# Layer norm roots in a macaron block: shift and Newton steps in place of ScalarE's square root

## The chip, the cores and the metric

The kernel runs on one core of a Trainium2 chip. The metric is the device time of one execution in microseconds (us). A core has five engines with an instruction stream of their own: TensorE (PE in the profile, with PEld for its weight loads), VectorE (DVE), ScalarE (ACT), GpSimd (POOL) and SyncE (SP), which issues most transfers.[...]

## The reference, cut to what matters

The block is a macaron: half a feed-forward network, causal attention, half a feed-forward network, each with a residual, on 8 sequences of 512 rows and 128 columns, all in float32. Each of the three parts begins with a layer norm, and the feed-forward part has a second one of its own directly behind the first.

```python
def _layernorm(x, eps=1e-05):
    m, v = mean(x, -1), var(x, -1)
    return (x - m) / sqrt(v + eps)

def ffn(x):                                  # 8 experts, 2 taken for each row
    xn = (x - mean(x)) * rsqrt(var(x) + eps) * ln_gamma + ln_beta
    abel = gelu(xn @ abel_w + abel_b)
    w = softmax over the top 2 of (xn @ gate_w + gate_b)
    moe = sum_e w[e] * (gelu(xn @ ew1[e] + eb1[e]) @ ew2[e] + eb2[e])
    for i in range(3): moe = moe @ expm(gens[i])
    gate = sigmoid([abel, moe] @ gc_w + gc_b)
    return x + abel * (1 - gate) + moe * gate

x = x + 0.5 * ffn(_layernorm(x))
x = x + attention(_layernorm(x))             # 16 heads of 8, causal, a bias by distance
x = x + 0.5 * ffn(_layernorm(x))
```

For each row the feed-forward part needs two roots of the same variance v: 1/sqrt(v + eps) for the outer norm, and 1/sqrt(v(1 + eps) + eps^2) for the two norms together. Attention needs the first alone. There are 8 x 512 rows, and each of the three parts takes its roots from new values of x.

## The kernel before, in words

A sequence is kept as a tile of 128 rows by 4 by 128 columns (`xs[b]`), so the statistics of one sequence are 4 numbers in each of the 128 partitions. The program has these stages, with the time that each begins in the profiled execution:

- 0 us, the prologue (`f_first`). `f_stats(0, ...)` makes the statistics of sequences 0 to 3 and then of 4 to 7 in one piece each (16 columns of variances). For each sequence `f_norm` normalises on VectorE (line 322), `f_turn` turns the tile on TensorE and scales it on ScalarE (lines 187 and 344), and `f_logits` makes the routing logits (`pl`, line 184). `f_sort` sorts rows by expert on VectorE, and `f_send` writes them to memory with indirect transfers that GpSimd issues (line 468). Between these runs `rotation_steps`, a chain of small matrix products (`rq`, `rc`, `rp`) that builds the matrix exponentials. TensorE's instructions are pinned to the order in which they are written (`mm`, `tp`, lines 183 to 187).
- 113 us, records of the experts' weights, and from 132 us the experts of sequences 0 to 3 (`f_experts(0, 0)`), their mixing (`f_fetch` with line 599's indirect transfers, `f_mix`), and the experts of sequences 4 to 7. Beside these last experts stand `statistics((0,), "o")` and `statistics((1,), "p")`, the attention norms of the first two sequences (the dictionary in `between`).
- 300 us, attention. One loop runs over slots; a unit is four heads of one sequence, 32 units of 12 slots. In each slot TensorE makes one score tile in each of two layouts: `sa`, of which VectorE takes the row maxima (line 925), and, 20 slots later for the same unit, `sb`, of which ScalarE takes exponentials (line 964). GpSimd zeroes what lies behind the diagonal (line 969, `affine_select`), and TensorE weighs the values (`py`). There are three buffers each of `sa` and `sb`, and two for everything else in TensorE's output memory. The dictionary `todo` puts other work into slots. `statistics` for sequences 2 to 7 ("q") is in slot 60. When a sequence is done, its feed-forward norm is put at 14 slots from there: `f_stats(1, (b,))` at 14, `f_norm` at 15 (on ScalarE, line 326), `f_turn` at 19, `f_half` at 21 and `f_logits` at 22. This is done for sequences 0 to 6, and the sends of group 0 follow on sequence 3's logits.
- 790 us, the second feed-forward part (`f_second`), which begins with `f_stats(1, (7,))` and then runs experts, fetches and mixing for both groups.

In `f_stats` the variances come from VectorE (lines 302 and 304), the two square roots from ScalarE (lines 305 and 306), the reciprocal of both, minus the mean times the root (`nm`) and two coefficients for the residual (`cf`) from VectorE again (lines 307 to 311). `statistics` has the same with one square root (lines 821 to 823). `f_norm`, `normalise` and `f_half` read these as scale and bias.

On ScalarE a function of another table set needs a load of the set. The square root is in a set that holds neither the exponential nor the gelu, so around each square root the program has a load before it and one behind it. A call to `pin` keeps the order among the instructions of an engine that are so marked; the rest is put in order by a scheduler of the framework.

Of the kernel before, what the change touches and what calls it, by code (L numbers as in the profile page):

```python
# [8 lines left out]
F32 = mybir.dt.float32  # L9
I32 = mybir.dt.int32  # L10
AF = mybir.ActivationFunctionType
ALU = mybir.AluOpType
# [4 lines left out]
P = 128  # L17
NB, S = 8, 512
# [6 lines left out]
EPS = 1e-5  # L25
# [31 lines left out]
def tile_macaron(  # L57
# [20 lines left out]
    V, A, G, T = nc.vector, nc.scalar, nc.gpsimd, nc.tensor  # L78

    const = ctx.enter_context(tc.tile_pool(name="const", bufs=1))  # L80
    stat = ctx.enter_context(tc.tile_pool(name="stat", bufs=2))
# [55 lines left out]

    ident = const.tile([P, P], F32, name="ident", tag="ident")
    make_identity(nc, ident)
    eps_c = const.tile([P, 1], F32, name="eps_c", tag="eps_c")  # L140
    G.memset(eps_c, EPS)
    eps2_c = const.tile([P, 1], F32, name="eps2_c", tag="eps2_c")
    G.memset(eps2_c, EPS * EPS)

    eye2 = early.tile([P, 2, P], F32, name="eye2", tag="eye2")
    for i in range(2):
# [34 lines left out]
    pin = tc.keep_in_program_order  # L181
# [105 lines left out]
    xTs = [const.tile([P, S], F32, name=f"xT{b}", tag=f"xT{b}") for b in range(NB)]  # L287
    made, xhs_f = {}, {}

    def f_stats(n, bs):  # L290


        name = f"{n}_{bs[0]}"
        w = len(bs) * TT
        st = stat.tile([P, w, 6], F32, name=f"st{name}", tag=f"st{w}")
        mv = stat.tile([P, w, 2], F32, name=f"mv{name}", tag=f"mv{w}")
        rs = stat.tile([P, 2, w], F32, name=f"rs{name}", tag=f"rs{w}")
        nm = stat.tile([P, w], F32, name=f"nm{name}", tag=f"nm{w}")
        cf = stat.tile([P, 2, w], F32, name=f"cf{name}", tag=f"cf{w}")
        for i, b in enumerate(bs):  # L300
            for t in range(TT):
                V.bn_stats(st[:, i * TT + t, :], xs[b][:, t, :])
        for t in range(w):
            V.bn_aggr(mv[:, t, :], st[:, t, :])
        A.activation(rs[:, 0, :], mv[:, :, 1], AF.Sqrt, bias=eps_c)
        A.activation(rs[:, 1, :], mv[:, :, 1], AF.Sqrt, bias=eps2_c, scale=1.0 + EPS)
        V.reciprocal(rs, rs)
        V.scalar_tensor_tensor(nm, mv[:, :, 0], -1.0, rs[:, 1, :], ALU.mult, ALU.mult)

        V.tensor_scalar(cf[:, 0, :], rs[:, 0, :], 0.5, 1.0, ALU.mult, ALU.add)  # L310
        V.scalar_tensor_tensor(cf[:, 1, :], mv[:, :, 0], -0.5, rs[:, 0, :], ALU.mult, ALU.mult)
        for i, b in enumerate(bs):
            made[n, b] = (rs, nm, cf, i * TT)
# [316 lines left out]
    def f_first(between):  # L630

        with ExitStack() as ph:
# [13 lines left out]
            groups = [tuple(range(g * GROUP, (g + 1) * GROUP)) for g in range(2)]  # L646
            go(1)
            f_stats(0, groups[0])
            go(2)
            for b in groups[0]:  # L650
# [6 lines left out]
            for b in groups[0]:  # L657
                f_half(0, b)
            go(1)
            f_stats(0, groups[1])  # L660
            go(1)
            for b in groups[1]:
# [37 lines left out]
    def f_second():  # L700

        with ExitStack() as ph:
            pools = f_pools(1, ph)
            n, b = 1, NB - 1
            sides = {b: f_beside(n, b, pools["hid"], pools["misc"], pools["sb"]) for b in range(NB)}

            def side(b):
                next(sides[b], None)

            tasks = {  # L710
                0: [(f_norm, n, b)],
                1: [(f_turn, n, b, pools["misc"])],
                2: [(f_logits, n, b, pools["misc"])],
                3: [(f_sort, n, 1, pools["misc"])],
                4: [(f_send, n, i, t) for i in range(GROUP, NB) for t in range(TT)],
                5: [(f_half, n, b)],
            }
            for i in range(NB):
                tasks.setdefault(5 + 2 * i, []).append((side, i))
                tasks.setdefault(6 + 2 * i, []).append((side, i))  # L720
            f_stats(n, (b,))
            f_experts(n, 0, pools, tasks)
            for b in range(GROUP):
                for t in range(TT):
                    f_fetch(n, b, t, pools["sb"], 2)
                f_mix(n, b, True)
            f_experts(n, 1, pools, {})
            for b in range(GROUP, NB):
                for t in range(TT):
                    f_fetch(n, b, t, pools["sb"], 2)  # L730
                f_mix(n, b, True)
# [78 lines left out]
    def statistics(bs, name):  # L810
        w = len(bs) * TT
        st = stat.tile([P, w, 6], F32, name=f"cst{name}", tag=f"cst{name}", bufs=1)
        mv = stat.tile([P, w, 2], F32, name=f"cmv{name}", tag=f"cmv{name}", bufs=1)
        rs = stat.tile([P, w], F32, name=f"crs{name}", tag=f"crs{name}", bufs=1)
        nm = stat.tile([P, w], F32, name=f"cnm{name}", tag=f"cnm{name}", bufs=1)
        for i, b in enumerate(bs):
            for t in range(TT):
                V.bn_stats(st[:, i * TT + t, :], xs[b][:, t, :])
        for t in range(w):
            V.bn_aggr(mv[:, t, :], st[:, t, :])  # L820
        A.activation(rs, mv[:, :, 1], AF.Sqrt, bias=eps_c)
        V.reciprocal(rs, rs)
        V.scalar_tensor_tensor(nm, mv[:, :, 0], -1.0, rs, ALU.mult, ALU.mult)
        for i, b in enumerate(bs):
            norms[b] = (rs, nm, i * TT)
# [58 lines left out]
    def attention():  # L884
# [4 lines left out]
        with ExitStack() as ph:  # L889
# [152 lines left out]
            for k in range(GROUP * TT):  # L1042
                b, t = GROUP + k // TT, k % TT
                at(2 + 3 * k, f_fetch, 0, b, t, work, 1)
                if t == TT - 1:
                    at(4 + 3 * k, f_mix, 0, b, False)
            before(1, NG * FILLS - 27)
            at(60, statistics, tuple(range(2, NB)), "q")
            for b in range(2, NB):
                before(b, b * NG * FILLS - 29)  # L1050
# [33 lines left out]
    def between(psum):  # L1084

        return {
            10: [(statistics, (0,), "o"), (normalise, 0)],
            13: [(turn, 0, psum)],
            15: [(spread, 0, 0, psum)],
            16: [(spread, 0, 1, psum)],  # L1090
            18: [(values, 0, psum)],
            20: [(statistics, (1,), "p")],
        }
# [87 lines left out]
```

## Time and profile before

| | |
|---|---|
| median of three runs | 1016.43 us (1006.78 to 1019.03) |
| the profiled execution's own time | 1012.17 us |
| its span, first to last instruction | 1010.1 us |
| mean granted TensorE clock | 0.860 |
| busy: TensorE, VectorE, ScalarE, GpSimd | 800.7, 546.6, 446.9, 348.7 us |
| table loads on ScalarE | 28, each 1.283 us (10 of them at line 305, 9 at line 964, 3 at line 821) |
| square roots on ScalarE | 23, of 0.28 to 0.32 us |

How to read the rows that follow: a row of the timeline has its start, its duration, the engine, the line, the operation, output and inputs by name, their shapes, how many instructions it holds, and in brackets the idle time before it with what ended it. A row of groups has the busy time, the mean of one in ns and then the idle time before. A row of windows has the window, its length, the busy time and the number of instructions of PE, PEld, DVE, ACT and POOL, and then the granted clock, the share of the DMA engines and GB/s.

### The profile page before, as it was taken

How to read it: one execution, taken by the hardware profiler on the slowest of the kernel's cores; microseconds unless marked ns; L12 is line 12 of the kernel's file. 1: busy time of each engine (PE TensorE's matmuls, PEld its weight loads, DVE VectorE, ACT ScalarE, POOL GpSimd, SP SyncE). 2: the span in 40 equal slices, each digit the busy share in tenths (PEclk: the TensorE clock that was granted, in tenths of full speed). 3: DMA queues.
4: the chain of work that ended last, by engine and by line, in shares of the span. 5: the costliest groups of instructions: out<-in, count | busy, mean ns of one | idle time of the engine just before them, and what ended most of it. 6: DMA issues, size and time to landing. Idle time of an engine off the chain costs nothing.

```text
span 1010.1 us, 17346 instructions
## 1 busy us (share of the span) xinstructions
PE 800.7 (79%) x5546; PEld 554.1 (55%) x5546; DVE 546.6 (54%) x2049; ACT 446.9 (44%) x928; POOL 348.7 (35%) x421
## 2 busy tenths in 40 slices
PE   4569888767668689999999967999999779956800
PEld 4469777656545345555555533455655578845800
DVE  5855533254338565676767672676773253445323
ACT  2434233235203355767676732666766434412300
POOL 4277700245034521121212138332111047074075
PEclk9579989978766777999999975999999789978955
DMA  9973166756621300101010101201000346766622
GB/s 259 299 188 75 56 224 221 217 158 178 159 71 25 69 14 11 36 4 43 4 44 3 44 17 49 56 10 42 4 3 2 107 148 217 248 178 179 218 58 68
DMA packets 104010, 101.22 MB, mean 100 GB/s; under 512 B 11424, under 2 KB 80936, under 8 KB 103640
## 3 DMA queue, kind: packets, MB, share of 16 engines
q1 hardware_dynamic: 95728, 83.26, 28.5%
q0 software_dynamic: 8192, 16.86, 6.0%
q8 instruction: 44, 0.72, 0.3%
q14 instruction: 46, 0.38, 0.1%
HBM read 34.37 MB, written 32.89 MB: 67 GB/s over the span
## 4 chain that ended last, share of the span: by engine, by line
PE 65%; DMA 8%; issue 7%; POOL 7%; DVE 7%; SPq 3%; ACT 2%; POOLq 0%; DVEq 0%; ACTq 0%
PE sa L184 18%; PE sb L184 9%; PE py L184 8%; POOL ye L599 6%; PE ph L184 6%; PE po L184 6%; DMA ye<-yd,to 4%; DMA xr<-xd 3%; PE rp L184 3%; PE pl L184 2%; PE pyt L187 2%; PE px L187 2%; PE pp L184 2%; SPq L509 1%; PE ab L184 1%
## 5 line engine op out<-in xcount | busy, mean ns | idle before, releaser
L925 DVE CUSTOM_DVE_ANT_0 junk<-sa,mask_q 128x128 f32<-128x128 f32 (+3 forms) x512 | 251.1, 490 | 146.1 <-PE sb L184 96.4
L184 PE MATMUL sa<-ks,qs 32*128 32x128 f32 (+3 forms) x1024 | 289.9, 514 | 15.4 <-DVE mx L925 15.2
L184 PE MATMUL sb<-qs,ks 32*128 32x256 f32 (+3 forms) x1024 | 284.8, 502 | 5.5 <-DMA qs<-mr 5.5
L964 ACT ACTIVATE pr<-sb 128x384 f32<-128x384 f32 (+1 forms) x384 | 188.6, 524 | 153.9 <-PE sb L184 142.7
L599 POOL DMA_INDIRECT ye<-yd,to x128 | 123.1, 961 | 239.5 <-DMA r<-rec 68.9
L184 PEld LDWEIGHTS sa<-ks,qs 32*128 32x128 f32 x1024 | 126.6, 203 | 117.8 <-DVE mx L925 88.4
L969 POOL TENSOR_SCALAR_AFFINE_SELECT pr<-pr 128x512 f32<-128x512 f32 x128 | 80.0, 637 | 302.5 <-ACT pr L964 302.4
L468 POOL DMA_INDIRECT xd<-xh,to x128 | 125.3, 979 | 110.3 <-issue 34.6
L546 ACT ACTIVATE hs<-ph,r 128x256 f32<-128x256 f32 x184 | 82.7, 474 | 151.9 <-PE ph L184 143.4
L184 PEld LDWEIGHTS sb<-qs,ks 32*128 32x128 f32 x1024 | 136.1, 199 | 18.3 <-issue 8.1
L184 PE MATMUL ph<-xs,r 128*128 128x256 f32 x368 | 113.5, 438 | 38.2 <-issue 24.4
L184 PEld LDWEIGHTS po<-r,hs 128*128 128x128 f32 x736 | 105.2, 208 | 6.0
L184 PE MATMUL po<-r,hs 128*128 128x129 f32 x736 | 104.5, 290 | 0.0
L184 PEld LDWEIGHTS ph<-xs,r 128*128 128x128 f32 x368 | 74.1, 224 | 48.4 <-issue 40.1
L184 PE MATMUL py<-pr,va 128*32 128x512 f32 (+3 forms) x1024 | 94.8, 469 | 2.8 <-POOL pr L969 2.8
L561 DVE TENSOR_TENSOR y<-po,r 128x258 f32<-128x258 f32 x92 | 39.0, 424 | 80.3 <-PE po L184 65.9
L532 DVE TENSOR_SCALAR xs<-px,cs 128x256 f32<-128x256 f32 x92 | 49.6, 541 | 53.9 <-PE px L187 51.5
L613 DVE TENSOR_TENSOR ye<-ye,wts 128x516 f32<-128x516 f32 x32 | 22.0, 696 | 91.2 <-DMA ye<-yd,to 91.2
L187 PE MATMUL px<-ident,xr 128*128 128x128 f32 x184 | 40.7, 308 | 38.0 <-DMA xr<-xd 32.3
L620 ACT ACTIVATE gt<-gt,half_gcb 128x4 f32<-128x4 f32 x16 | 4.7, 296 | 114.9 <-DVE gt L619 114.9
L184 PEld LDWEIGHTS py<-pr,va 128*32 128x32 f32 x1024 | 24.4, 112 | 53.9 <-issue 23.0
L187 PEld LDWEIGHTS px<-ident,xr 128*128 128x128 f32 x184 | 24.1, 156 | 50.2 <-issue 31.8
(185 smaller groups left out, 850.2 us busy)
## 6 DMA issues: line engine op xcount, KB each, us to landing
r<-rec SPq DMA_DIRECT2D x92, 322.5 KB
yd<-y SPq DMA_DIRECT2D x92, 129.0 KB
xr<-xd SPq DMA_DIRECT2D x92, 128.0 KB
xd<-blank SPq DMA_DIRECT2D x2, 2944.0 KB
qkd<-qk SPq DMA_DIRECT2D x16, 256.0 KB
x<-in_x_dram SPq DMA_DIRECT2D x8, 256.0 KB
qs<-in_alibi_q_dram SPq DMA_DIRECT2D x2, 1024.0 KB
ks<-in_alibi_k_dram SPq DMA_DIRECT2D x2, 1024.0 KB
```

The lines of the kernel that those rows point to most:

```text
L184: pin(T.matmul(*args, **kw))
L187: pin(T.transpose(*args))
L468: d = G.indirect_dma_start(out=xd[g], out_offset=bass.IndirectOffsetOnAxis(to[:, k, j : j + 1], 0), in_=xhs_f[n, b][:, t, :], in_offset=None,)
L509: e = nc.sync.value_load(whose[0:1, t : t + 1], min_val=0, max_val=NE - 1)
L532: V.tensor_scalar(xT, pt.rearrange("p c q -> p (c q)"), cs[:, C_GAMMA : C_GAMMA + 1], cs[:, C_BETA : C_BETA + 1], ALU.mult, ALU.add,)
L546: A.activation(got[t][3][:, c, :], ph[:, :SLOTS], AF.Gelu, bias=r[:, E_B1 + c : E_B1 + c + 1])
L561: V.tensor_tensor(y, po, r[:, E_B2:RECORD].unsqueeze(1).to_broadcast([P, CHUNKS, PO]), ALU.add)
L599: pin(G.indirect_dma_start(out=back[b][k][:, t, :], out_offset=None, in_=yd[g], in_offset=bass.IndirectOffsetOnAxis(to[:, k, j : j + 1], 0),))
L613: V.tensor_tensor(ys[k], ys[k], wts[:, k, js].unsqueeze(2).to_broadcast([P, TT, PO]), ALU.mult)
L925: V.tensor_tensor_reduce(junk[:, :n], sa[:, at : at + n], mask_q[:, S - n :], 1.0, -3.0e38, ALU.add, ALU.max, mxs[u][:, j, i : i + 1],)
L964: A.activation(pr[:, j, :], sb[:, :width], AF.Exp)
L969: pin(G.affine_select(out=pr[:, :, at : at + P], in_=pr[:, :, at : at + P], pattern=[[0, GH], [1, P]], compare_op=ALU.is_ge, fill=0.0, bas ...
```

## The change

Both square roots go. A new helper, `inverse_root`, takes the variance with eps added and makes 1/sqrt of it: it shifts the number's bits right by one, takes that from the constant 1597463007 (as a multiplication by -1 and an addition, into an integer), and reads the bits as a number again. Three Newton steps follow, each y = y(1.5 - 0.5 v y^2), written as four instructions. The two integer instructions are on VectorE always. The twelve others are on VectorE too, or, where `late` is set, on GpSimd and pinned there. `late` is set for `f_stats(1, (b,))` with b from 0 to 6, the seven calls within attention. The constant tiles `eps_c` and `eps2_c` go, as do the reciprocals; eps is added by a `tensor_scalar` on VectorE. In `statistics` the result is copied into `rs`.

```diff
-    eps_c = const.tile([P, 1], F32, name="eps_c", tag="eps_c")
-    G.memset(eps_c, EPS)
-    eps2_c = const.tile([P, 1], F32, name="eps2_c", tag="eps2_c")
-    G.memset(eps2_c, EPS * EPS)
...
+    def inverse_root(v, name, late):
+        shape, key = list(v.shape), "x".join(str(d) for d in v.shape[1:])
+        y = stat.tile(shape, F32, name=f"iy{name}", tag=f"iy{key}")
+        t = stat.tile(shape, F32, name=f"it{name}", tag=f"it{key}", bufs=1)
+        V.tensor_scalar(y.bitcast(I32), v.bitcast(I32), 1, None, ALU.logical_shift_right)
+        V.tensor_scalar(y.bitcast(I32), y.bitcast(I32), -1.0, 1597463007.0, ALU.mult, ALU.add)
+        E, keep = (G, pin) if late else (V, lambda i: i)
+        for _ in range(3):
+            keep(E.tensor_tensor(t, y, y, ALU.mult))
+            keep(E.tensor_tensor(t, t, v, ALU.mult))
+            keep(E.tensor_scalar(t, t, -0.5, 1.5, ALU.mult, ALU.add))
+            keep(E.tensor_tensor(y, y, t, ALU.mult))
+        return y
...
     def f_stats(n, bs):
...
-        rs = stat.tile([P, 2, w], F32, name=f"rs{name}", tag=f"rs{w}")
+        ve = stat.tile([P, 2, w], F32, name=f"ve{name}", tag=f"ve{w}", bufs=1)
...
-        A.activation(rs[:, 0, :], mv[:, :, 1], AF.Sqrt, bias=eps_c)
-        A.activation(rs[:, 1, :], mv[:, :, 1], AF.Sqrt, bias=eps2_c, scale=1.0 + EPS)
-        V.reciprocal(rs, rs)
+        V.tensor_scalar(ve[:, 0, :], mv[:, :, 1], 1.0, EPS, ALU.mult, ALU.add)
+        V.tensor_scalar(ve[:, 1, :], mv[:, :, 1], 1.0 + EPS, EPS * EPS, ALU.mult, ALU.add)
+        rs = inverse_root(ve, f"f{name}", n == 1 and len(bs) == 1 and bs[0] < NB - 1)
...
     def statistics(bs, name):
...
-        A.activation(rs, mv[:, :, 1], AF.Sqrt, bias=eps_c)
-        V.reciprocal(rs, rs)
+        V.tensor_scalar(ve, mv[:, :, 1], 1.0, EPS, ALU.mult, ALU.add)
+        rs = stat.tile([P, w], F32, name=f"crs{name}", tag=f"crs{name}", bufs=1)
+        V.tensor_copy(rs, inverse_root(ve, f"c{name}", False))
```

More of the change, by code (lines that the diff above doesn't have):

```diff
@@ L813, in statistics @@
         mv = stat.tile([P, w, 2], F32, name=f"cmv{name}", tag=f"cmv{name}", bufs=1)
-        rs = stat.tile([P, w], F32, name=f"crs{name}", tag=f"crs{name}", bufs=1)
+        ve = stat.tile([P, w], F32, name=f"cve{name}", tag=f"cve{name}", bufs=1)
         nm = stat.tile([P, w], F32, name=f"cnm{name}", tag=f"cnm{name}", bufs=1)
```

## The prediction

> **What bounds the kernel now.** I read the page's summary and chain first, then the stages, then every place where a square root stands.
>
> ```profile
> PE 800.7 (79%) x5546; PEld 554.1 (55%) x5546; DVE 546.6 (54%) x2049; ACT 446.9 (44%) x928; POOL 348.7 (35%) x421
> PE 65%; DMA 8%; issue 7%; POOL 7%; DVE 7%; SPq 3%; ACT 2%; POOLq 0%; DVEq 0%; ACTq 0%
> ```
>
> TensorE makes 65% of the chain, ScalarE 2%: work taken off ScalarE is worth little unless TensorE waits for it. By stage:
>
> ```profile
> core 0: us, PE busy (x) PEld busy (x) DVE busy (x) ACT busy (x) POOL busy (x), PEclk, DMA share, GB/s
> 400.00:580.00 180.00, 180.00 (x1484) 100.62 (x1483) 123.55 (x519) 125.45 (x259) 36.87 (x56) 1.00 0.11 26
> 640.00:790.00 150.00, 149.98 (x1232) 83.00 (x1230) 91.92 (x384) 99.59 (x206) 35.43 (x53) 0.99 0.08 19
> ```
>
> In attention TensorE is full at full clock. Seven of the ten layer norm roots stand there, one for each of sequences 0 to 6. The trace around one of them:
>
> ```profile
> 411.65 1.28 ACT L305 ACT_TABLE_LOAD   x1
> 412.19 0.36 DVE L304 BATCH_NORM_AGGREGATE mv<-st 128x2 f32<-128x6 f32 x4
> 412.94 0.30 ACT L305 ACTIVATE rs<-mv,eps_c 128x4 f32<-128x4 f32 x1
> 413.44 1.28 ACT L964 ACT_TABLE_LOAD   x1
> 413.66 0.20 DVE L307 RECIPROCAL rs<-rs 128x8 f32<-128x8 f32 x1
> 413.89 0.16 DVE L308 SCALAR_TENSOR_TENSOR nm<-mv,rs 128x4 f32<-128x4 f32 x1
> 414.74 0.60 ACT L964 ACTIVATE pr<-sb 128x512 f32<-128x512 f32 x1
> 415.23 1.64 ACT L326 ACTIVATE xh<-x,nm,rs 128x128 f32<-128x128 f32 x4
> ```
>
> The first load overlaps VectorE's variances; nm is ready at 414.05, but xh starts only at 415.23, behind the second load and an exponential. ScalarE is shut to exponentials from 411.65 to 414.72. At sequence 6 this reaches TensorE:
>
> ```profile
> 760.19 0.29 PEld L184 LDWEIGHTS sb<-qs,ks 32*128 32x128 f32 x2 [0.34 <-ACT pr L964]
> 761.07 0.42 PEld L187 LDWEIGHTS pt<-ident,xh 128*128 128x128 f32 x4 [0.59 <-ACT mr L937]
> ```
>
> ```profile
> 758.60:762.10 3.50, 3.50 (x17) 1.73 (x16) 1.54 (x10) 3.24 (x10) 0.74 (x2) 1.00 0.00 0
> 762.10:765.50 3.40, 3.40 (x32) 2.09 (x30) 0.57 (x2) 1.52 (x3) 0.29 (x1) 0.50 0.04 7
> ```
>
> The clock column falls from 1.00 to 0.50 for 3.4 us after these short waits: attention has little slack there.
>
> **The change part by part.** *Removed:* 24 of 28 table loads (4 are left in the built program) and 23 square roots, 24 x 1.28 + 23 x 0.30 = 38 us of ScalarE. Some of it already reaches TensorE: its waits on ScalarE around the seven roots are some 1.3 us at six of them and 2.9 at sequence 6, 10.7 us in all, the most that quick roots can return. *Added:* thirteen chains of two integer operations and 12 Newton steps: six chains wholly on VectorE (the two groups of the prologue, sequence 7, and the three of statistics), seven with their 12 steps on GpSimd. TensorE's order stays as it was, and SyncE's transfers only swap among neighbours.
>
> *Prologue.* The roots of sequences 4 to 7 are on the chain:
>
> ```profile
> 43.55 1.07 DVE L304 BATCH_NORM_AGGREGATE mv<-st 128x2 f32<-128x6 f32 x15
> 45.52 0.33 DVE L307 RECIPROCAL rs<-rs 128x32 f32<-128x32 f32 x1
> 45.88 0.18 DVE L308 SCALAR_TENSOR_TENSOR nm<-mv,rs 128x16 f32<-128x16 f32 x1
> 46.82 0.87 PE L187 MATMUL pt<-ident,xh 128*128 128x128 f32 x3 [3.81 <-DVE xh L322]
> ```
>
> Here the square roots cost nothing: they ran at 44.65 to 45.16 beside three rotation products on VectorE. In their place come 16 dependent VectorE operations of 0.19 (the 128x32 row of lg) + 0.035 of spacing (413.86 to 413.89) = 3.6 us, less 0.35 for the reciprocal: +3.1 (a little of it may hide). For sequences 0 to 3, six of the steps are put ahead of VectorE's copies that TensorE's first rotation products wait for at 11.23: +1.1. TensorE is full behind this (37.69 of 38 us from 75 to 113), so +4.2 stays.
>
> *Attention, seven times.* VectorE: two scalings and two integer operations, 4 x 0.165, end 0.65 after mv, about 413.2 (no shift of integers is in the trace; the nearest rows with an int32 result are 0.167 and 0.206, so 0.65 to 0.8). Then come a hand-over of 0.1, 12 steps of price p on GpSimd, a hand-over back, nm (0.16) and the hand-over to ScalarE: xh starts at 413.6 + 12p, in place of 415.23. No tiny arithmetic on GpSimd is in the trace; the nearest rows:
>
> ```profile
> L835 POOL TENSOR_TENSOR x<-x,rw 128x512 f32<-128x512 f32 x8 | 10.2, 1279 | 0.0
> L755 POOL TENSOR_SCALAR_AFFINE_SELECT steps_q<-steps_q 32x512 f32<-32x512 f32 x1 | 0.6, 604 | 0.0
> L151 POOL TENSOR_SCALAR_AFFINE_SELECT mask_q<-mask_q 128x128 f32<-128x128 f32 x1 | 0.3, 283 | 0.0
> ```
>
> From 604 and 283 ns for 512 and 128 columns follows 176 ns at no columns; 8 columns at the tensor_tensor's 2.15 ns each make 0.19, with VectorE's spacing p = 0.225, 12p = 2.7, and xh is 1.1 later: 7 x 1.1 = +7.8. Below, the memset of one column took 97 ns: p = 0.10 gives -0.4 each, -2.6 in all. Above, p = 0.30 gives +2.0 each, +14. I take 0.225, the rows nearest in kind. The Trainium skill (GPSIMD Engine Reference, 4.1 Engine selection) speaks against this placing: elementwise work belongs on VectorE, being about twice as slow on GpSimd for two inputs. Twice VectorE's row here (0.165) is p = 0.33 and +2.4 each, +17 in all; but that factor is of long rows, and in these the start of an operation is nearly all, so the rows decide.
>
> The new wait is nm's: VectorE stands some 2.7 us for GpSimd. Behind it are queued cf, the four va additions and the score maxima (L925) of the next sa tiles; TensorE waits for these when the three sa buffers are used up, and turns xh only after xh. ScalarE meanwhile does the exponentials that it could not do before; xh is queued in front of later ones, so they wait too. GpSimd itself is not behind: the affine_select that follows the chain waited 6.59 us for ScalarE at 415.46, and only sequence 4's chain has a send (0.98 us) just before it. This cover holds the stall to about xh's shift; without it up to 2.5 us each would show.
>
> *The clock.* Stalls of 2 us come in each of the seven places; before, the one of this size was followed by a half-clock window of 3.4 us, worth 1.7. Half of the six others: 3 x 1.7 = +5.1 (ends 0 and 10.2). The Trainium skill (TensorE: Matmul & The Clock Gate, Why this matters for your kernels) asks only for gaps under about 3 us; by it this term is 0 and the total 12.5. The row at 762.10 fell after gaps under 0.6 us each, so I keep it.
>
> *The rest.* In statistics "o" and "p" lie beside gathers and mixing: +0.25. "q" gives exponentials 2.6 us and takes 3.4 us of VectorE in a stretch with idle engines: 0 (-1 to +1). The last f_stats, on VectorE: nm 0.8 later, xh mostly hidden by expert products: +0.3 (0.2 to 0.8). If the exponentials' freed time returned one third of the 10.7, that would be -3.6; I don't count it, since nm's wait stands in the same place.
>
> Sum: 4.2 + 7.8 + 5.1 + 0.25 + 0.3 = +17.6. Against the profiled execution's own 1012.17 (span 1010.1 and 2.1 around it) that is 1029.8; against the median shown, 1016.43, it is 1034.0. I say 1032. About 2%, 20 us, is what a measurement of this kernel can tell from no change: faster is under 996.1, slower over 1036.8.
>
> **The rivals.** *Main, 0.42:* as summed, 1032; its own range is 1020 (p = 0.15, no clock) to 1045 (p = 0.30, all six windows). *The clock stays down, 0.28:* after a wait of 3.86 us at 366.57 the clock was half from 366.1 to 390.0, 24 us, worth 12. If the stalls of nm add to the waits for sa and xh so that one window falls under what sequence 6 had, each such place costs 12 in place of 1.7; two or three of seven make 17.6 + 18 to 36, some 1050. The point: TensorE stands more than about 3 us in one place. For it: at sequence 6 it was near already. Against it: many weights stay ready ahead. *Cheap steps, 0.22:* p about 0.15, no new half-clock windows: 4.2 + 1.6 + 0.8 = +6.6, 1021. *A gain, 0.08:* p = 0.10 and the freed ScalarE returns the 10.7: 4.5 - 10.7 = -6, 1010. For it: exponentials really are shut out for 3.1 us each time; against it: xh waits for a longer chain. That the loads stay is excluded, since the built program has four.
>
> The range 1011 to 1052 leaves out half of the gain and somewhat under half of the slow rival, 0.16. Slower by over 2%: all of the rival and a third of the main case, 0.41; faster by over 2% needs more than everything returned, 0.02; within 0.57.
>
> **What would show it.** ScalarE with 4 table loads; the GpSimd steps with their mean (0.19 expected) and VectorE's nm waiting 2.7 us on GpSimd seven times; the first pl of sequence 4 at about 53.6 in place of 49.37; weight loads of pt and sa waiting 1 to 2 us after each f_stats; in 400 to 790, a few 3.4 us windows at half clock. Wrong if p is far from 0.2, if TensorE's pt is far enough behind xh to hide the shift, or if half-clock stretches come of the moved timing alone.

## The result, and the profile after

The changed kernel took 1059.12 us (median of four, 1054.67 to 1064.83), the kernel before beside it 1011.61: a ratio of 1.0467, interval 1.037 to 1.0563. It is slower by 47 us where 16 to 18 were forecast, and lies above the stated range. Medians are of all runs of a kernel, but ratios and intervals, here and below, compare only those within 1.5% of the kernel's fastest, so a ratio can differ from that of the two medians. The profiled execution has a span of 1058.1 us and a mean clock of 0.831 (before 0.860).

The page's summary, its chain by engine, and from the groups of ScalarE the table loads of the kernel after:

```profile
PE 827.3 (78%) x5546; PEld 571.6 (54%) x5546; DVE 564.8 (53%) x2160; ACT 411.4 (39%) x881; POOL 365.1 (34%) x503
PE 60%; POOL 10%; DVE 9%; DMA 9%; issue 8%; ACT 2%; SPq 1%; POOLq 0%; DVEq 0%; ACTq 0%
```

```profile
L215 ACT ACT_TABLE_LOAD x1 | 1.3, 1283 | 0.8 <-PEq L1177 0.8
L496 ACT ACT_TABLE_LOAD x1 | 1.3, 1283 | 0.0
L977 ACT ACT_TABLE_LOAD x1 | 1.3, 1283 | 0.0
L558 ACT ACT_TABLE_LOAD x1 | 1.3, 1283 | 0.0
```

The change did what it says: four loads are left, and ScalarE is 35 us less busy. TensorE, with the same instructions, is 27 us more busy. The two stages of attention that were full at full clock before, in the table by stage of the kernel after:

```profile
400.00:580.00 180.00, 173.81 (x1340) 97.57 (x1344) 113.71 (x473) 102.50 (x221) 40.84 (x87) 0.91 0.09 20
640.00:790.00 150.00, 142.65 (x1085) 78.41 (x1085) 89.91 (x375) 78.00 (x165) 55.12 (x90) 0.87 0.11 27
```

The granted clock fell from 1.00 and 0.99 to 0.91 and 0.87, and TensorE now has gaps there. Laying the same TensorE instruction of both traces side by side shows where the time is lost: 8.0 us by 71 us (the prologue), 4.0 from 390 us of the kernel before to sequence 0's root (a stretch at half clock in front of that took 13.7 us and not 23.9), 44.9 at the end of sequence 7, 48 at the end. So attention lost 40.8 us, and it did so at each of the seven roots (3.6 to 8.2 us). One of them, in the timeline of the kernel after:

```profile
416.25 0.36 DVE L316 BATCH_NORM_AGGREGATE mv<-st 128x2 f32<-128x6 f32 x4
...
417.12 0.17 DVE L293 TENSOR_SCALAR iyf<-iyf 128x8 int32<-128x8 int32 x1
...
417.38 0.20 POOL L296 TENSOR_TENSOR itf<-iyf 128x8 f32<-128x8 f32 x1 [4.46 <-DVE iyf L293]
417.65 0.20 POOL L297 TENSOR_TENSOR itf<-itf,ve 128x8 f32<-128x8 f32 x1
...
420.49 0.20 POOL L299 TENSOR_TENSOR iyf<-iyf,itf 128x8 f32<-128x8 f32 x1
420.65 0.64 POOL L982 TENSOR_SCALAR_AFFINE_SELECT pr<-pr 128x512 f32<-128x512 f32 x1
420.73 0.57 DVE L320 SCALAR_TENSOR_TENSOR nm<-mv,iyf 128x4 f32<-128x4 f32 x1 [2.84 <-POOL iyf L299]
...
421.33 1.65 ACT L338 ACTIVATE xh<-x,nm,iyf 128x128 f32<-128x128 f32 x4 [3.60 <-DVE nm L320]
421.37 0.87 DVE L889 TENSOR_TENSOR va<-pv,rw 128x128 f32<-128x128 f32 x4
...
422.35 0.09 PEld L183 LDWEIGHTS pm<-ident,mx 128*16 128x16 f32 x1 [2.10 <-issue]
...
422.38 0.27 PE L183 MATMUL pm<-ident,mx 128*16 128x128 f32 x1 [1.73 <-DVE va L889]
```

Twelve steps on GpSimd, each 0.20 long and 0.283 from the next, take 3.31 us. VectorE stands 2.84 us for them, and nm itself takes 0.57 in place of 0.16. From the end of mv to the end of nm it is 4.69 us (before 1.50, from 412.55 to 414.05). Behind nm stand the four va additions, and for the last of them pm waits, the transpose of the maxima. It doesn't wait for maxima: those that it turns were finished at 417.9. It waits for a buffer. Of the two buffers that pm can use, one holds py, which is still being summed, and the other pv, which the va additions read. In the kernel before they end at 415.03, and pm comes 1.5 us later without a wait for them:

```profile
414.14 0.89 DVE L876 TENSOR_TENSOR va<-pv,rw 128x128 f32<-128x128 f32 x4
416.53 0.09 PEld L187 LDWEIGHTS pm<-ident,mx 128*16 128x16 f32 x1 [0.33 <-issue]
```

At sequence 6 there is no pv, and there the row maxima behind nm are what TensorE waits for (kernel after):

```profile
802.35 0.52 PEld L180 LDWEIGHTS sa<-ks,qs 32*128 32x128 f32 x4 [2.78 <-DVE mx L938]
```

And then the clock, by windows of 3.41 us:

```profile
414.74:418.16 3.42, 3.42 (x26) 1.51 (x24) 3.01 (x17) 1.19 (x2) 0.60 (x3) 1.00 0.39 65
418.16:421.57 3.41, 2.49 (x26) 1.12 (x26) 0.84 (x5) 0.24 (x1) 2.40 (x10) 1.00 0.11 12
421.57:424.98 3.41, 2.29 (x13) 1.35 (x13) 2.88 (x17) 3.16 (x9) 0.07 (x1) 1.00 0.00 0
424.98:428.40 3.42, 3.42 (x26) 2.11 (x30) 1.19 (x6) 1.71 (x3) 0.56 (x1) 0.50 0.01 2
428.40:431.81 3.41, 3.41 (x23) 3.09 (x16) 1.32 (x5) 2.39 (x7) 0.00 (x0) 0.50 0.00 0
431.81:435.22 3.41, 3.41 (x19) 2.23 (x19) 1.76 (x6) 1.18 (x3) 0.74 (x2) 0.50 0.00 0
```

Two windows in which TensorE was busy for 2.49 and 2.29 of 3.41 us are followed by three at half clock. The theory to test: the wait of nm on GpSimd holds what is queued behind it on VectorE, TensorE stalls by about 2 us, and the half clock that follows costs more than the stall. (The expectations below still speak of the row maxima behind nm; at sequences 0 to 5 it is the va additions.)

### The profile page after: what moved, and what is told of

It is laid out like the page before. It is cut to its first block, busy times and chain, and to the rows that moved or that the text cites. A ratio compares the mean times of both kernels' runs of the same rounds, so it can differ in the third digit from the quotient of the medians.

```text
span 1058.1 us, 17420 instructions
## 1 busy us (share of the span) xinstructions
PE 827.3 (78%) x5546; PEld 571.6 (54%) x5546; DVE 564.8 (53%) x2160; ACT 411.4 (39%) x881; POOL 365.1 (34%) x503
## 4 chain that ended last, share of the span: by engine, by line
PE 60%; POOL 10%; DVE 9%; DMA 9%; issue 8%; ACT 2%; SPq 1%; POOLq 0%; DVEq 0%; ACTq 0%
PE sa L180 15%; PE sb L180 8%; PE py L180 7%; PE ph L180 6%; POOL ye L611 6%; PE po L180 5%; DMA ye<-yd,to 4%; DMA xr<-xd 3%; PE rp L180 3%; PE pl L180 2%; POOL xd L480 2%; PE pyt L183 2%; PE px L183 2%; PE pp L180 2%; DVE junk L938 1%
## 5 line engine op out<-in xcount | busy, mean ns | idle before, releaser
L180 PE MATMUL sa<-ks,qs 32*128 32x128 f32 (+3 forms) x1024 | 301.3, 533 | 19.3 <-DVE mx L938 19.3
L180 PE MATMUL sb<-qs,ks 32*128 32x512 f32 (+3 forms) x1024 | 296.5, 523 | 7.7 <-DMA qs<-mr 6.7
L180 PEld LDWEIGHTS sa<-ks,qs 32*128 32x128 f32 x1024 | 130.1, 209 | 124.2 <-DVE mx L938 91.5
L180 PEld LDWEIGHTS sb<-qs,ks 32*128 32x128 f32 x1024 | 143.3, 210 | 21.3 <-issue 9.1
L180 PE MATMUL py<-pr,va 128*32 128x512 f32 (+3 forms) x1024 | 97.6, 482 | 2.1 <-POOL pr L982 2.1
```

The source lines that it names most:

```text
L180: pin(T.matmul(*args, **kw))
```

## The experiments

The runs of this section were made on three chips: one for attn_only, attn_sqrt, all_vector and pool_nm, one for the three with "pin" in their name and one_step, one for the others. On the first two the kernel before takes some 1140 us, since engines stand there for up to 32 us at single instructions, mostly outside attention, with no releaser that the profile names; the cause is open. Each ratio is to the kernel before on the same chip, and the lengths of sequences within attention agree between chips (53.22 us in the kernel before and in attn_sqrt). The traces of attn_only, all_vector and two_steps are of executions well above the shortest of their runs (1188.98, 1190.64 and 1059.9 us for 1170.4, 1161.64 and 1041.13), so a shorter one may hold less half clock.

For each run three things are read around the roots of sequences 0, 1 and 2 (sequence 3 is followed by a sort, which brings half-clock windows in every kernel): the waits of TensorE's weight loads, summed over those longer than 0.25 us from 4 to 15 us after the transposes that end a sequence (pyT), or up to the fall of the clock where it fell sooner, since a lower clock brings waits of its own; the time at half clock; and the length of the sequence.

| run | hold of VectorE before nm, us | waits, us | half clock, us | length, us | ratio to before |
|---|---|---|---|---|---|
| kernel before | none on GpSimd | 3.5 | 0, 0, 0 | 53.2 to 53.4 | 1 |
| attn_sqrt | none | 3.5 | 0, 0, 0 | 53.2 | 1.0065 |
| one_step | 0.57 | 3.5 | 0, 0, 0 | 53.1 to 53.5 | 1.0157 |
| vec_two | none | 3.5 | 0, 0, 0 | 53.2 | 0.9968 |
| two_steps | 1.69 | 4.3, 3.7, 4.3 | 0, 13.7, 10.2 | 54.2, 60.0, 59.0 | 1.0305 |
| all_vector | none (busy) | 5.0, 4.6, 4.5 | 10.2, 6.8, 6.8 | 59.3, 58.2, 57.7 | no interval |
| pool_nm | none | 5.3, 4.6, 4.9 | 3.4, 13.7, 6.8 | 56.5, 60.9, 58.5 | 1.0568 |
| changed kernel | 2.84 | 5.8, 5.2, 5.3 | 10.2, 6.8, 13.7 | 59.7, 58.4, 61.4 | 1.0467 |
| six_steps | 5.4 | 7.3, 5.3, 5.8 | 20.5, 17.1, 10.2 | 66.8, 64.4, 62.2 | 1.0883 |

**The parts of the change.** attn_only changes only the seven roots in attention; attn_sqrt changes all others.

The edit of attn_only against the changed kernel:

```diff
+        if n == 1 and len(bs) == 1 and bs[0] < NB - 1:
+            V.tensor_scalar(ve[:, 0, :], mv[:, :, 1], 1.0, EPS, ALU.mult, ALU.add)
...
+        else:
+            rs = stat.tile([P, 2, w], F32, name=f"rs{name}", tag=f"rs{w}")
+            A.activation(rs[:, 0, :], mv[:, :, 1], AF.Sqrt, bias=eps_c)
...
-        V.tensor_copy(rs, inverse_root(ve, f"c{name}", False))
+        A.activation(rs, mv[:, :, 1], AF.Sqrt, bias=eps_c)
+        V.reciprocal(rs, rs)
```

attn_sqrt has the condition negated, and statistics as in the changed kernel.

> Only the seven roots within attention are changed (the prologue's, sequence 7's and the three of statistics keep ScalarE's square root). Theory (the wait of nm on VectorE costs about 5.7 us at each of seven places, some 3 to 4 of it in half-clock windows): 1012 + 40 = 1052, half-clock time in attention up by about 60 us. Rival (the prologue and the other roots carry half of the loss): 1030 to 1035.

> The reverse: the seven roots within attention go back to ScalarE's square root, all others are by bits and Newton steps on VectorE. Theory: 1012 + 7 = 1019, all of it behind the prologue's second group of roots. Rival: 1035 to 1040.

attn_only: 1183.06 us against 1140.73, ratio 1.0348 (1.0284 to 1.0413), which is 39.7 us, and 42.3 at the medians. attn_sqrt: 1147.45, ratio 1.0065 (1.0028 to 1.0103), 6.7 us at the medians. Both fell where the theory put them, and the rival is more than 10 us off in both. The two parts make 1.041, against 1.047 and, in the repetition below, 1.050 for the whole, within the intervals. The loss is in attention.

**The engine of the steps.** all_vector sets `late` to False everywhere.

> The twelve steps of the seven roots in attention run on VectorE too. VectorE is then busy for about 2.4 us in front of nm where it stood idle for 2.84 us, nm takes 0.16 and not 0.57 us, so nm ends 0.8 us earlier. Theory (what counts is how late the row maxima behind nm come): stall of TensorE at the maxima's transpose down from 1.7 to about 0.9 us, fewer half-clock windows, 1030 to 1045. Rival (GpSimd itself, its port or its queue, is the cause): back to 1019 to 1022. Rival (the amount of time does not matter, each hold brings the half clock): 1055.

The four runs took 1161.64 to 1199.65 us (median 1186.0), too far apart for an interval, but all above the highest of the kernel before (1146.62) and 9 us or more above what the rival with GpSimd as the cause would give. So GpSimd is not the cause as such: with the steps on VectorE, 0.20 us apart, nm came 0.7 us sooner, the stall at pm fell from 2.1 to 0.8 us (it ends with the va additions here too), and half-clock windows came all the same. My theory had expected fewer of them, and in the trace there are about as many (10.2, 6.8 and 6.8 us for 10.2, 6.8 and 13.7 of the changed kernel). The shortest run, 1.8% over the kernel before, is where the theory puts it; the other three (3.6 to 5.2%) are above that, about where the rival is in which any hold brings the half clock (4.2%). Between these two the run does not decide.

**The wait taken off VectorE.** pool_nm makes nm and cf on GpSimd:

```diff
-        V.scalar_tensor_tensor(nm, mv[:, :, 0], -1.0, rs[:, 1, :], ALU.mult, ALU.mult)
...
+            V.tensor_scalar(nh[:, 0, :], mv[:, :, 0], -1.0, None, ALU.mult)
+            V.tensor_scalar(nh[:, 1, :], mv[:, :, 0], -0.5, None, ALU.mult)
+            pin(G.tensor_tensor(nm, nh[:, 0, :], rs[:, 1, :], ALU.mult))
+            pin(G.tensor_scalar(cf[:, 0, :], rs[:, 0, :], 0.5, 1.0, ALU.mult, ALU.add))
+            pin(G.tensor_tensor(cf[:, 1, :], nh[:, 1, :], rs[:, 0, :], ALU.mult))
```

> In the seven roots within attention nm and the two cf are made on GpSimd behind the Newton steps (VectorE only scales the mean beforehand), so VectorE no longer waits for GpSimd; xh comes at the same time or 0.3 us later than in the changed kernel. Theory (the row maxima queued behind nm): the 40 us of attention go, 1010 to 1022. Rival (the late xh and the exponentials queued behind it on ScalarE): 1045 to 1060.

1199.59 us, ratio 1.0568 (1.0498 to 1.0638), more even than the rival's 1.033 to 1.047: the theory in this form fell. The timeline, and the waits of the weight loads, of pool_nm:

```profile
553.45 1.65 ACT L346 ACTIVATE xh<-x,nm,iyf 128x128 f32<-128x128 f32 x4 [3.37 <-POOL nm L324]
...
555.00 1.22 ACT L985 ACTIVATE pr<-sb 128x384 f32<-128x384 f32 x3
```

```profile
552.93 0.09 PEld L183 LDWEIGHTS pm<-ident,mx 128*16 128x16 f32 x1 [0.34 <-issue]
555.52 0.49 PEld L180 LDWEIGHTS sb<-qs,ks 32*128 32x128 f32 x2 [1.86 <-ACT pr L985]
```

The wait at pm is back at 0.34 us, since the va additions no longer stand behind nm. But xh stands 3.37 us at the head of ScalarE's queue with exponentials behind it, so the sb buffers are not freed and TensorE waits 1.86 us one step later. Two in-order queues have a reader of the root at their head, and ScalarE's alone is enough. (VectorE's alone was not run; in the changed kernel the wait seen at pm is VectorE's.)

**Both readers freed.** pool_nm_pin also moves xh behind three more exponentials; best_pin keeps ScalarE's root outside attention; before_pin has the moves without any change of roots.

```diff
-                A.activation(pr[:, j, :], sb[:, :width], AF.Exp)
+                pin(A.activation(pr[:, j, :], sb[:, :width], AF.Exp))
...
-                    at(done + 15, f_norm, 1, b)
-                    at(done + 19, f_turn, 1, b, ps_x)
-                    at(done + 21, f_half, 1, b)
-                    at(done + 22, f_logits, 1, b, ps_x)
+                    at(done + 18, f_norm, 1, b)
+                    at(done + 22, f_turn, 1, b, ps_x)
+                    at(done + 24, f_half, 1, b)
+                    at(done + 25, f_logits, 1, b, ps_x)
```

(xh is pinned too, and the sort of group 0 goes from 24 to 27.)

> As the run with nm and cf on GpSimd, and xh is moved behind three more exponentials on ScalarE (its slot from 15 to 18, turn, half and logits three slots later too, exponentials and xh kept in program order), so that neither VectorE nor ScalarE stands for the Newton steps. Theory now (each in-order queue that holds the chain's reader stops TensorE by about 2 us, and this, not the chain, brings the half clock): no half-clock windows at the seven places, TensorE's waits there at or under the 4.25 us of before, ratio to before 0.997 to 1.007 with the prologue's +7 us still in it. Rival (GpSimd's steps in front of the affine_selects, or the moved timing alone, bring the half clock): ratio 1.035 to 1.06.

> As the run just before, with ScalarE's square root kept in the prologue, in statistics and for sequence 7. Theory: 7 us less than that run, ratio to before 0.99 to 1.00; it is below 1 only if the loads within attention cost something before (at most 10.7 us, 1%).

> The kernel before, with only the moves of xh, turn, half and logits by three slots and the program order on ScalarE; all roots by ScalarE's square root. Control for the two runs before it: if they gain by the moves and not by the missing table loads, this gains as much (0.99 to 1.00). Theory: 1.00, since before no reader stood for the roots for more than 0.6 us.

Ratios 1.0247 (1.0179 to 1.0315), 1.0169 (1.0092 to 1.0246) and 1.0108 (1.0032 to 1.0185). The first lies between the theory and the rival. About the roots the waits fell to some 2.9 us in all three, as the theory said, but half-clock windows came in some sequences all the same, 17.5 to 18.7 us behind the transposes, in the control too. In front of them the weights of the moved logits wait; the row from before_pin:

```profile
493.05 0.97 PEld L184 LDWEIGHTS pl<-gw,xT 128*128 128x128 f32 x8 [0.76 <-issue]
```

That this wait brings the fall is not shown. In before_pin the waits of sequences 0 and 1 are the same up to there, 0.30 and 0.76 us behind those at the root, and the clock fell for 13.7 us in sequence 0 and not at all in sequence 1. What is shown is that the moves alone can bring it, and that they cost 1% of their own; against the control, which has all the table loads, best_pin is not faster (17.8 us above the kernel before, the control 14.2; the intervals overlap). The forecast of 0.99 to 1.00 for it was wrong, and so was 1.00 for the control. What can be read: with both readers freed, more than half of pool_nm's loss is gone (2.5% in place of 5.7%, on another chip).

**The length of the chain.** In the seven roots, `for _ in range(3)` becomes 1, 2 or 6 where `late` is set. One step leaves roots good to 0.2% only, two to 5e-6.

> The changed kernel with one Newton step in place of three in the seven roots within attention (roots only good to 0.2%). The chain on GpSimd is 1.1 us and not 3.4, VectorE stands about 0.6 us in front of nm and not 2.84. Theory (a threshold: waits of TensorE about a root up to 4.25 us in all did not touch the clock, 5.3 and more did): no half clock, +7 to +9 us, ratio 1.006 to 1.010. Rival (loss in proportion to the hold): +7 + 0.2 x 40 = +15 us, 1.013 to 1.016. Rival (GpSimd's share of the work itself): 1.035 to 1.05.

> Two Newton steps in the seven roots within attention (good to 5e-6). VectorE's hold in front of nm falls from 2.84 to about 1.7 us. Theory (threshold between 3.5 and 4.2 us of TensorE's waits about a root): the waits are about 4.5 us, so half-clock windows come at most places, but the stall is 1 us each and not 2.3; 1.025 to 1.035. Rival (loss in proportion to the hold): 1.006 + 0.6 x 0.035 = 1.027, too near to tell by the time, but then with half-clock windows at about half of the places.

> Six Newton steps in place of three in the seven roots within attention (the roots are no different). The hold of VectorE goes from 2.84 to 6.2 us. Theory: the stalls grow by 3.4 us each, 24 us in all, and the half clock is there already, so it adds 0 to 3 us each: ratio to before 1.06 to 1.085. Rival (the loss is the half clock alone, brought by any hold): as three steps.

> The changed kernel as it is, beside the kernel before on the chip of this call, where the kernel before takes some 1140 us. If the two parts add up (attention 42 us and the rest 7 us there), 1.040 to 1.046.

one_step: 1155.01 us, ratio 1.0157 (1.0069 to 1.0246). By the time alone this is what the rival in proportion to the hold forecast (1.013 to 1.016), above my 1.006 to 1.010. The trace has nothing of it at the roots. nm and the wait of pm there, from two views of one_step:

```profile
496.40 0.16 DVE L320 SCALAR_TENSOR_TENSOR nm<-mv,iyf 128x4 f32<-128x4 f32 x1 [0.57 <-POOL iyf L299]
```

```profile
498.52 0.09 PEld L183 LDWEIGHTS pm<-ident,mx 128*16 128x16 f32 x1 [0.34 <-issue]
```

The hold of 0.57 us is covered, the waits are the 3.5 us of before, and no sequence but 3 and 6 has a window at half clock, as before. The traced execution is the shortest of four, 1148.6 us, 9.4 above the kernel before. Two others took 1161 and 1162 us, and no trace shows where; so the trace speaks against the rival, and the median does not exclude it.

two_steps: 1052.9, ratio 1.0305 (1.0201 to 1.0408). six_steps: 1104.63, ratio 1.0883 (1.079 to 1.0976). after_again: 1064.73 against 1015.67, ratio 1.0502 (1.0407 to 1.0598), a little over the 1.040 to 1.046 expected. The table above gives the dose: at waits of 3.5 us in all there is no half clock (12 sequences of 12 in the four rows), from 3.7 to 4.3 there mostly is (at five of sequences 0 to 5 of two_steps, but once at 4.3 and in vec_two twice at 3.7 not), at 4.5 and more always 3.4 us or more. two_steps came as the theory had it, six_steps a little over, as its stall brings 10 to 20 us of half clock and not the 7 to 14 of three steps. In it the wait of pm is

```profile
427.87 0.09 PEld L183 LDWEIGHTS pm<-ident,mx 128*16 128x16 f32 x1 [5.06 <-issue]
```

From three repetitions of three steps (the changed kernel twice and attn_only), the length of a sequence by its half-clock time: 58.3 to 58.4 us with 6.8, 59.6 to 59.7 with 10.2, 61.1 to 61.4 with 13.7. That is 0.42 us lost for each us at half clock, and 55.5 us at none: a stall of 2.3 us over 53.2, which is just what the waits of sequence 0 grew by (5.8 less 3.5).

**A chain short enough.** vec_two keeps ScalarE's root everywhere but in attention, and there takes two steps of three instructions on VectorE:

```diff
+            V.tensor_scalar(h, v, -0.5, None, ALU.mult)
+            for _ in range(2):
+                V.tensor_tensor(t, y, y, ALU.mult)
+                V.tensor_tensor(t, t, h, ALU.mult)
+                V.scalar_tensor_tensor(y, t, 1.5, y, ALU.add, ALU.mult)
```

> The seven roots within attention on VectorE with two Newton steps of three instructions (seven small instructions behind the two integer ones, no hand-over); all other roots by ScalarE's square root. nm comes about as early as with one step on GpSimd, where no half clock was seen. Theory: 0.996 to 1.002, the candidate for the best version. Rival (VectorE's added 1.4 us of work holds the maxima enough to bring the half clock): 1.02 to 1.03.

The median is 1015.99 us against 1015.67, the ratio 0.9968 (0.9933 to 1.0003): no difference from the kernel before can be told, and it is 4.6% below the 1064.73 of the changed kernel. But five of its twenty runs (1026 to 1038 us) are longer than the longest of the 23 of the kernel before (1024.49), and what happens in these no trace shows. The groups of its table loads, and the waits at a root:

```profile
L335 ACT ACT_TABLE_LOAD x3 | 3.8, 1283 | 9.6 <-DVE mv L328 9.5
L995 ACT ACT_TABLE_LOAD x2 | 2.6, 1283 | 0.0
```

```profile
413.64 0.09 PEld L187 LDWEIGHTS pm<-ident,mx 128*16 128x16 f32 x1 [0.34 <-issue]
415.24 0.42 PEld L187 LDWEIGHTS pt<-ident,xh 128*128 128x128 f32 x4 [0.59 <-ACT mr L968]
```

The seven loads on each side within attention are gone, nm ends 2.58 us after mv, and the waits are what they were with the loads: 3.5 us, sequence length 53.2. The va additions end 1.05 us later than in the kernel before, and pm comes no later: in the kernel before it came 1.5 us behind them. Taking the loads away returned nothing that can be told.

## Why the prediction was wrong

The direction and the place were right, the size was not: +47 us for +17.6. The step that failed most is the clock, which was taken for half of the places and one window each and came at every place, with two to four windows more at six of the seven; next the stall, 2.3 us at each root in place of 1.1. By its steps:

- *What the removed loads return.* Counted at nothing in the sum, 10.7 us at most. It is nothing that can be told: one_step and vec_two have no loads there and the same 3.5 us of waits, though in one_step xh starts 0.6 us sooner than before. The waits that the trace put down to ScalarE were not the loads' doing: the 0.59 us of pt ends with mr, the copy of pm that frees pm's buffer, and stands in vec_two too.
- *The price of a step.* 0.225 us was taken, 0.283 measured, so 3.31 us for 2.7. The Trainium skill's factor of two (GPSIMD Engine Reference, 4.1 Engine selection) would have given 0.33; against VectorE's 0.20 in all_vector it is 1.4, between the row's estimate and the rule.
- *nm.* Taken at 0.16; it took 0.57 in all seven places, and in all of attn_only, after_again and six_steps, and each time it began 0.08 us into the affine_select that follows the chain on GpSimd and ended with it to 0.01 us. In one_step and two_steps, where the affine_select came later, it took 0.16.
- *The stall.* "xh is 1.1 later: 7 x 1.1 = +7.8" was mis-sized: from the end of mv to xh it is 4.72 us where it was 2.68, so xh is 2.0 later; over the forecast the price of a step adds 0.7 and nm 0.4, and shorter hand-overs take back 0.2. The stall was 2.3 us at each place, 16 in all. "This cover holds the stall to about xh's shift" came near by the number, but not by the path, so that is luck: pt waits for pm's buffer, not for xh. The prediction named the va additions and the maxima behind nm, but for the three sa buffers; it did not name pm, nor the buffer that va frees for it. nm came 3.2 us later, the additions with it, the cover was 1.4 (the 1.5 less a hand-over of 0.1), and pm came 1.8 later; another 0.5 is the wait of sa for the maxima behind it.
- *The clock.* This is the larger one: "Half of the six others: 3 x 1.7 = +5.1". Every place got 6.8 to 13.7 us more at half clock (3.4 at sequence 6). From sequence 0's root to the end of attention there were 102.3 us at half clock where before there were 37.5; at 0.42 us for one, the 65 us are 27. "Half" had no reason beside it, and the one case it rested on was misread: sequence 6 was taken for a stall of 2 us, but by the measure of the table its waits up to the fall were 3.8 us, 0.3 more than at the six places that kept the clock there. The Trainium skill's rule (TensorE: Matmul & The Clock Gate, Why this matters for your kernels), gaps under about 3 us, would have given 0; here the longest single wait was 2.2 us at sequences 0 to 5 (2.8 at 6), in two_steps 0.84 up to the fall at sequences 1 to 5, a wait that every kernel has there, and the clock fell. Several shorter waits within some ten microseconds were enough.
- *The prologue.* +4.2 forecast, +3.6 at the first pt of sequence 4, 3.1 at its first pl (52.46, not 53.6) and 8.0 by 71 us, since a stretch at half clock ran from 46 to 70 us and not from 45 to 56; the clock of the prologue was put at nothing. That 4.0 is left at the start of attention, near the 4.2, is luck: a later half-clock stretch was shorter. VectorE's chain is 3.3 us longer (from mv to nm 5.65 in place of 2.33), as worked out; of the 1.1 us of the first group only 0.5 was left at the second. The rows of the kernel after:

```profile
44.05 1.07 DVE L316 BATCH_NORM_AGGREGATE mv<-st 128x2 f32<-128x6 f32 x15
49.70 0.18 DVE L320 SCALAR_TENSOR_TENSOR nm<-mv,iyf 128x16 f32<-128x16 f32 x1
52.46 1.88 PE L180 MATMUL pl<-gw,xT 128*128 128x8 f32 x8 [0.87 <-ACT xT L356]
```

- *The rivals.* The slow rival, 1050 with 0.28, named the mechanism, but its point of decision was wrong: it asked for more than 3 us in one place and for 24 us of half clock at two or three. It came as some 10 us at each of seven.

The sum as measured: 16 of stalls and 27 of half clock make 43, where attention lost 40.8 in the trace; with 4.0 that stood at its beginning and 3.1 behind it that is the 48 of the two spans. The excess of 2 us comes, it seems, of carrying the fit of three sequences to all seven. What is not settled is what TensorE's gate counts. Around the roots the runs give a range of waits (3.7 to 4.3 us before the fall) between not and always, not its rule. Counted over all fourteen traces within attention, by pairs of 3.41 us windows at full clock: where such waits filled 4.25 us or more of a pair, a half-clock window followed 20 times of 20; under 3.5 us it followed 36 times of 1101, 13 of them in the three pinned runs. So waits of this size are enough, but they are not the only thing that lowers the clock.

## What to carry to other kernels

A chain of dependent small operations on another engine is paid where its result is read: look for every in-order queue that has a reader at its head, and count the delay for the work queued behind each reader (here the additions behind nm, which free a buffer, and the exponentials behind xh), not for the reader alone. Freeing one queue moves the stall to the next. In a stretch where TensorE is full at full clock, price a stall of 2 us at two to three times its length (here 40.8 us for 16) until a run shows that the clock holds, and don't count a table load as gain unless TensorE is seen to wait for it and to stop waiting without it.

## What the runs showed of the hardware that was not expected

A VectorE operation of 128 x 4 elements with two tensor inputs took 0.57 us in place of 0.16 when it began inside a GpSimd affine_select, and ended with it (28 of 28 in four traces). An arithmetic operation of 128 x 8 elements on GpSimd took 0.20 us, with 0.08 to the next; on VectorE 0.17 with 0.03. And the granted clock fell to one half after stretches in which no single wait of TensorE's weight loads was longer than 0.84 us (two_steps, sequences 1 to 5), when the waits up to there, from 4 us behind the transposes on, were 3.7 to 4.3 us in all.
